# Masked layers of a cross-attention stack: a piece of work moves ahead of the scores in the pairs that follow a use of the scores' banks

## The chip, the cores and the metric

The kernel runs on one core of a Trainium2 chip. The metric is the device time of one execution in microseconds. Before the change the median of three runs is 4831.26 us (4831.16 to 4831.56). One more execution was profiled; its own time is 4829.9 us, and its span from the first to the last instruction is 4828.2 us. All work is in fp32, apart from a small bias term in bf16.

## The reference

The input is x with 2048 rows (queries) of 256 values, and a context of 1601 rows of 512 values. Four layers follow each other, and each adds to x what attention over the same context gives. Layers 0, 2 and 3 ("masked") have 16 heads of 64:

```
q = x @ Wq;  k = ctx @ Wk;  v = ctx @ Wv            # split into 16 heads of 64
logits = q k^T / 8 + col_bias                        # col_bias: up to -20 in four columns, by query
probs = softmax(logits)                              # over the 1601 keys
x = x + (probs v) @ Wo + bo
```

Layer 1 ("grouped") normalises x first and has 16 query heads of 16 values that share 4 key and value heads. The change does not touch its arithmetic.

## The kernel before

**Tiling.** A masked layer is cut into 8 blocks of two heads. In a block the 2048 queries are cut into 4 units of 512. So a masked layer has 32 units, and the three of them have 96. A unit works through the 1601 keys in 13 chunks (12 of 128 keys and one of 65). One chunk of one unit is a step. The scores of a step are keys by queries, for two heads: a tile of 128 x 1024 that fills two PSUM banks. The pool of these tiles (`psum.pair`, called `s` in the profile) has two of them.

**Three stages at once.** The main loop (line 1155) takes two steps at a time, which the text calls a pair. In a pair, three units are at work in different stages. For the newest one, `masked_scores` (line 681) computes scores on TensorE (L687, and L694 for the bias of the last chunk), ScalarE copies them to SBUF (L699), and VectorE keeps a running maximum over the chunks (L702 and L704, called `top`). Both read the tile of the scores, and the tile is free when both have done so. When a unit's 13 chunks are through, `maxima` (line 740) transposes the running maximum on TensorE into another tile of the scores' pool (L747), VectorE reduces it (L748), and two transfers spread the result over all partitions. For the unit before, 18 steps behind its scores, VectorE subtracts the maxima (L778), ScalarE takes exps (L783), and GpSimd adds them up (L786, L788). Its maxima are loaded into a PSUM tile by `maxima_spread` (L773) when it starts. Two steps behind the exps, `values` (line 808) multiplies by v on TensorE (L823).

**Pieces.** Everything else is cut into pieces that are put between the pairs (class `Pieces`, line 966). Each has a cost, and says whether it uses the PSUM bank that pieces share (`pm`). The fill pieces compute keys (L440) and values (L394) of the next block, 14 for a block of 26 pairs; each is followed by ScalarE's copy out of `pm`. Due pieces have a step at which they must run. A unit's queries (L464) are due at step 11 of the unit before. When a unit's values are complete, at step 6 of the second unit after it, `finish` (line 886) makes three more due: the denominators (L844 transposes the sums, L848 reduces them) two steps later, the division on GpSimd (L864) five steps later, and the project (L872, added to x by L884) ten steps later. Denominators and project use no `pm`, but a tile of the scores' pool; they are the ones that are marked `shared=False`.

`pair` (line 990) chooses for a pair of steps: it runs what is due (`own`, line 980), and if that cost nothing it takes one fill piece. The order of a pair in the program before is: the subtractions, the scores with copies and maxima, the exps, the values, then the pieces, and `maxima` where a unit's scores end. In the pair where a unit's values end on the first step, half of the values stands behind the piece.

**What sets the order.** The last lines of the function (1208 to 1214) chain the instructions of TensorE, ScalarE and VectorE in the order in which the program writes them. GpSimd and the queue of SyncE, which issues nearly all transfers, are not in that chain.

Two units take 26 steps, 13 pairs. In them two maxima, two denominators and two projects take a tile of the scores' pool.

Of the kernel before, what the change touches and what calls it, by code (L numbers as in the profile page):

```python
# [32 lines left out]

@with_exitstack
def tile_cross_attention_stack(ctx: ExitStack, tc: tile.TileContext, t: dict, out: bass.AP):

# [29 lines left out]
    x, cond = t["x"], t["ctx_2048"]  # L68
# [8 lines left out]
    NT = len(TCH)  # L77
# [22 lines left out]
    class Scores:  # L100
# [16 lines left out]
        def pair(self, shape=(2, QB)):  # L117
            return self.pairs.tile([P, *shape], FP, name="s")
# [40 lines left out]
    def key_order(tok):  # L159
# [27 lines left out]
        first = const.tile([P, NTOK], FP, name="first")  # L187
        keep = small.tile([P, NTOK], FP, name="keep", bufs=1)
        nc.vector.tensor_tensor(pair, across(tok), along(tok), ALU.is_equal)
        nc.vector.tensor_tensor(pair, pair, before, ALU.mult)  # L190
        nc.vector.tensor_reduce(first, pair, AX.X, ALU.max)
        nc.vector.tensor_scalar(first, first, 0.0, None, ALU.is_equal)
        nc.vector.scalar_tensor_tensor(first, tok, 0.0, first, ALU.is_ge, ALU.mult)
# [18 lines left out]
        def sources(a, b):  # L212
            n = b - a
            wide = [P, n, NTOK]

            def tokens_of(v):
                return v.rearrange("p (o j) -> p o j", o=1).to_broadcast(wide)

            def at_positions(v):
                return v.rearrange("p (n o) -> p n o", o=1).to_broadcast(wide)  # L220

            test = probs.tile(wide, FP, name="p")
            spec = probs.tile([P, n], FP, name="p")
            place = probs.tile([P, n], FP, name="p")
            to, at = src[:, a:b], pos[:, a:b]
            nc.vector.tensor_tensor(test, at_positions(at), tokens_of(where), ALU.is_ge)
            nc.vector.tensor_reduce(to, test, AX.X, ALU.add)
            nc.vector.tensor_tensor(to, to, at, ALU.add)

            nc.vector.tensor_scalar(place, at, count, float(T), ALU.add, ALU.subtract)  # L230
            nc.vector.scalar_tensor_tensor(to, place, 0.0, to, ALU.is_lt, ALU.mult)
            nc.vector.tensor_tensor(test, at_positions(place), tokens_of(rank), ALU.is_equal)
            nc.vector.tensor_tensor(test, test, tokens_of(mine), ALU.mult)
            nc.vector.tensor_reduce(spec, test, AX.X, ALU.add)
            nc.vector.tensor_tensor(to, to, spec, ALU.add)
# [713 lines left out]
    def first_unit(i):  # L949

        if i < NT / 2:
            first_block(i)
        if i == 1:
            layers[0].load_wo(made[0, 0])
            for b in range(NB):
                keep(0, b)
                pieces.at(2 * i + 2 + 2 * b, [(0, biases[b])])
        if i == 3:
            token_marks(0)
        if i == 7:  # L960
            small_constants()
            for l in range(1, NL):
                token_marks(l)
            start_block(0)

    class Pieces:
# [4 lines left out]
        def __init__(self):  # L971
            self.fill, self.later = deque(), deque()
            self.due = {}
            self.credit = 0.0

        def at(self, step, found):
            for steps, piece in found:
                self.due.setdefault(step + steps, []).append(piece)

        def own(self, steps):  # L980

            cost, taken = 0.0, False
            for step in steps:
                for piece in self.due.pop(step, ()):
                    piece.run()
                    cost += piece.cost
                    taken |= piece.shared and piece.cost > 0
            return cost, taken

        def pair(self, steps, pairs):  # L990

            cost, taken = self.own(steps)
            many = len(self.fill) + len(self.later) > pairs
            while self.fill and not taken and (many or not cost):
                piece = self.fill.popleft()
                piece.run()
                cost += piece.cost
                taken = piece.shared and piece.cost > 0

        def steps(self, steps, share):  # L1000


            self.credit = max(min(self.credit + share, 2.5), -2.5)
            cost, taken = self.own(steps)
            self.credit -= cost
            while self.fill and not taken and self.credit >= self.fill[0].cost / 2:
                piece = self.fill.popleft()
                piece.run()
                self.credit -= piece.cost
                taken = piece.shared and piece.cost > 0  # L1010
# [13 lines left out]
    pieces = Pieces()  # L1024
# [127 lines left out]
    def masked(unit):  # L1152
        return unit and unit.masked

    for first in range(0, N + NT + DELAY + LAG + 16, 2):
        pair = [Step(first), Step(first + 1)]

        if any(masked(x.scoring) for x in pair):
            if psum.banks:
                psum.by_pairs()  # L1160
        elif pair[0].exping and not pair[0].exping.masked and not psum.banks:
            psum.singly()

        kn, cn = divmod(first + 2 - NT - DELAY, NT)
        ahead = of[kn] if cn == 0 and 0 <= kn < len(units) and of[kn].masked else None
        three = not ahead and not any(masked(x.exping) for x in pair)
        for x in pair:
            x.begin()
        for x in pair:
            if masked(x.exping):  # L1170
                if x.cb == 0 and x is pair[1]:
                    x.exping.maxima_spread()
                x.exping.subtract(x.cb)
        for x in pair:
            if masked(x.scoring):
                x.scoring.masked_scores(x.ca)

        ends = all(masked(x.valuing) for x in pair) and pair[0].cv == NT - 1
        if ends:
            pair[0].valuing.values(NT - 1)  # L1180
        for x in pair:
            if masked(x.exping):
                x.exping.masked_exp(x.cb)
        if ahead:
            ahead.maxima_spread()
        if not ends:
            for x in pair:
                if masked(x.valuing):
                    x.valuing.values(x.cv)
        first_unit(first // 2)  # L1190
        together = masked(pair[0].scoring) and (masked(pair[1].exping) or not pair[1].exping)
        for x in pair:
            x.grouped(three)
            x.end()
            if not together:
                pieces.steps([x.step], x.share())
        if together:
            pieces.pair([first, first + 1], round(pair[0].units_left() * NT / 2))
        if ends:
            pair[1].valuing.values(0)  # L1200
        for x in pair:
            if x.scoring and x.ca == NT - 1:
                x.scoring.maxima()
                if not x.scoring.masked:
                    pieces.at(first + 2, [(0, Piece(x.scoring.maxima_rows, 0.3))])

# [41 lines left out]
```

## Time and profile before

| what | value |
|---|---|
| median of three runs | 4831.26 us |
| profiled execution: own time, span | 4829.9 us, 4828.2 us |
| TensorE matmul busy | 4667.0 us, 97% of the span |
| VectorE, ScalarE, GpSimd busy | 3746.8, 3225.1, 2991.6 us |
| idle TensorE ahead of scores L687 | 82.9 us |
| mean granted TensorE clock | 0.981 of full speed |

The masked layers take the profile from the start to about 1260 us and from about 2290 us to the end; between them lies the grouped layer. In the profile `s` is a tile of the scores' pool, `p` a tile of scores or probabilities in SBUF, `b` the maxima as `maxima_spread` puts them into PSUM, `pm` the bank of the pieces, `po` the values' output. A line of the timeline gives the start, the duration, the engine, the line of the kernel, the operation and its tiles, how many instructions are merged (x), and in brackets how long the engine was idle before and who released it. PEld is TensorE's weight load. A line of waits gives the total in us, how often, and the longest.

### The profile page before, as it was taken

Reading aid. Unit: us, or ns where it says so; the run is one execution under the profiler, and the core shown is the slowest. Engines: PE = TensorE matmul, PEld = TensorE weight load, DVE = VectorE, ACT = ScalarE, POOL = GpSimd, SP = SyncE. Lnnn points to the kernel's source line nnn. Section 1 sums busy time; section 2 is a strip of 40 time slices with the busy share of each in tenths; the row PEclk is TensorE's granted clock in tenths of the full one; section 3 lists DMA queues with packets and bytes.
Section 4 is the critical chain, followed back from the end, with each engine's and each line's share of the span. In section 5 each row is a group of like instructions: output and inputs, shape, how many; then the busy total and the mean of one; then the engine's idle time right before and its main releaser. Section 6 shows DMA issues by size and latency. Waiting matters only on the chain.

```text
span 4828.2 us, 64072 instructions
## 1 busy us (share of the span) xinstructions
PE 4667.0 (97%) x24020; PEld 1949.9 (40%) x24020; DVE 3746.8 (78%) x3766; ACT 3225.1 (67%) x4010; POOL 2991.6 (62%) x1440
## 2 busy tenths in 40 slices
PE   8999999999999999999999999999999999999996
PEld 5444444443433333343444444444444444444432
DVE  5888888888766666652678888888888888888886
ACT  5777777777545555544677777777777777777774
POOL 3777777778620000000577777777777777777787
PEclk9999999999889999998999999999999999999998
DMA  5322322222210000021232322322232222223201
GB/s 156 85 80 79 88 74 85 83 81 78 66 33 22 26 21 21 23 56 29 67 97 74 85 83 83 84 80 84 75 92 74 85 79 85 81 79 89 72 29 35
DMA packets 345990, 337.75 MB, mean 70 GB/s; under 512 B 112425, under 2 KB 301353, under 8 KB 345680
## 3 DMA queue, kind: packets, MB, share of 16 engines
q1 hardware_dynamic: 341984, 328.28, 23.8%
q8 instruction: 189, 3.10, 0.3%
q0 software_dynamic: 1152, 3.28, 0.2%
q10 hardware_dynamic: 2544, 2.10, 0.1%
q14 instruction: 121, 0.99, 0.1%
HBM read 318.76 MB, written 14.69 MB: 69 GB/s over the span
## 4 chain that ended last, share of the span: by engine, by line
PE 87%; DVE 10%; issue 1%; POOL 1%; ACT 1%; DMA 0%; POOLq 0%; ACTq 0%; DVEq 0%; SPq 0%
PE po L823 28%; PE s L687 20%; PE t L718 9%; PE pm L394 7%; PE pm L440 6%; PE s L872 4%; PE pm L464 4%; DVE ntop L748 2%; DVE rden L848 2%; PE s L844 2%; DVE xs L884 2%; PE s L747 2%; DVE top L704 1%; POOL sums L788 1%; PE t L793 1%
## 5 line engine op out<-in xcount | busy, mean ns | idle before, releaser
L788 POOL TENSOR_TENSOR sums<-sums,p 128x1024 f32<-128x1024 f32 (+1 forms) x1152 | 2726.4, 2367 | 741.0 <-ACT p L783 569.9
L699 ACT COPY p<-s 128x1024 f32<-128x1024 f32 (+1 forms) x1248 | 1234.7, 1014 | 665.7 <-PE s L687 573.5
L823 PE MATMUL po<-p,v 128*64 128x512 f32 (+3 forms) x8320 | 1506.7, 528 | 8.8 <-ACT p L783 5.8
L778 DVE TENSOR_TENSOR p<-p,b 128x1024 f32<-128x1024 f32 (+1 forms) x1248 | 1461.3, 1209 | 55.2 <-ACT b L773 52.9
L704 DVE TENSOR_TENSOR top<-s,top 128x1024 f32<-128x1024 f32 (+1 forms) x1056 | 1291.1, 1223 | 239.7 <-ACT p L699 176.7
L687 PE MATMUL s<-q,kT 64*128 64x512 f32 (+1 forms) x4992 | 1342.9, 632 | 82.9 <-DVE ntop L748 23.8
L783 ACT ACTIVATE p<-p 128x1024 f32<-128x1024 f32 (+1 forms) x1248 | 1254.8, 1057 | 49.1 <-DVE p L778 47.7
L823 PEld LDWEIGHTS po<-p,v 128*64 128x64 f32 (+3 forms) x8320 | 366.9, 126 | 1138.9 <-issue 905.4
L687 PEld LDWEIGHTS s<-q,kT 64*128 64x128 f32 (+1 forms) x4992 | 390.2, 182 | 721.1 <-issue 217.1
L805 ACT ACTIVATE p<-t 128x512 f32<-128x512 f32 (+1 forms) x760 | 413.7, 594 | 337.3 <-PE t L793 300.5
L731 DVE TENSOR_REDUCE row_top<-t 128x1 f32<-128x512 f32 x700 | 451.2, 686 | 215.7 <-PE t L793 186.6
L864 POOL TENSOR_TENSOR oT<-oT,by 128x512 f32<-128x512 f32 x112 | 142.9, 1276 | 719.4 <-DMA by<-cols 427.0
L793 PE MATMUL t<-q,kT 32*128 32x512 f32 (+1 forms) x1520 | 496.6, 656 | 0.0
L718 PE MATMUL t<-kT,q 32*128 32x512 f32 (+1 forms) x1880 | 490.1, 563 | 0.0
L394 PEld LDWEIGHTS pm<-wv,ct 128*128 128x128 f32 (+1 forms) x2600 | 300.4, 187 | 131.0 <-issue 68.4
L394 PE MATMUL pm<-wv,ct 128*128 128x128 f32 (+2 forms) x2600 | 333.3, 281 | 2.2 <-ACT v L398 0.9
L440 PE MATMUL pm<-ct,wk 128*128 128x256 f32 (+1 forms) x1344 | 314.5, 377 | 1.1 <-ACT ct L273 1.1
L748 DVE TENSOR_REDUCE ntop<-s 128x8 f32<-128x1024 f32 x96 | 117.6, 1225 | 232.8 <-PE s L747 232.8
L440 PEld LDWEIGHTS pm<-ct,wk 128*128 128x128 f32 x1344 | 230.8, 190 | 156.5 <-issue 101.0
L718 PEld LDWEIGHTS t<-kT,q 32*128 32x128 f32 x1880 | 183.7, 187 | 161.0 <-issue 94.1
L872 PE MATMUL s<-oT,wo 128*128 128x512 f32 x392 | 199.1, 631 | 15.1 <-POOL oT L864 11.1
L786 POOL COPY sums<-p 128x1024 f32<-128x1024 f32 x96 | 99.7, 1038 | 176.0 <-ACT p L783 176.0
(152 smaller groups left out, 2310.3 us busy)
## 6 DMA issues: line engine op xcount, KB each, us to landing
ct<-ctxT SPq DMA_DIRECT2D x288, 512.0 KB
xT<-xT SPq DMA_DIRECT2D x100, 512.0 KB
spread<-cols SPq DMA_DIRECT2D x96, 512.0 KB
by<-cols SPq DMA_DIRECT2D x192, 128.0 KB
xT<-xs SPq DMA_DIRECT2D x16, 512.0 KB
ct<-ctxT SPq DMA_DIRECT2D x48, 130.0 KB
wk<-in_L_xattn_Wk_dram SPq DMA_DIRECT2D x24, 256.0 KB
wv<-in_L_xattn_Wv_dram SPq DMA_DIRECT2D x24, 256.0 KB
```

What stands on the lines that cost most here:

```text
L394: nc.tensor.matmul(pv[:md, d, :f], ct(k)[:, d * P : d * P + md], wv[:, k, :], start=(k == 0), stop=(k == NCT - 1),)
L440: nc.tensor.matmul(pk, u.wk[:, k, :], ct(k), start=(k == 0), stop=(k == NCT - 1))
L687: nc.tensor.matmul(s[:m, h, :], self.u.kT[r, a : a + m], self.q[r, :], start=True, stop=(a != TAIL),)
L699: nc.scalar.copy(p[:m], s[:m])
L704: nc.vector.tensor_tensor(self.top[:m], s[:m], self.top[:m], ALU.max)
L718: nc.tensor.matmul(s[:, at : at + n], self.q[r, ts(q, P)], self.u.kT[r, a : a + n], start=True, stop=True,)
L731: nc.vector.tensor_reduce(self.top[:, of, q, k : k + 1], s, AX.X, ALU.max)
L778: nc.vector.tensor_tensor(self.p[c][:m], self.p[c][:m], self.less[:m], ALU.add)
L783: nc.scalar.activation(p[:m], p[:m], AF.Exp)
L788: nc.gpsimd.tensor_tensor(self.sums[:m], self.sums[:m], p[:m], ALU.add)
L793: nc.tensor.matmul(s[:m], self.u.kT[r, a : a + m], self.q[r, :], start=True, stop=True)
L823: nc.tensor.matmul(to, v, p, start=(c == 0 and not part), stop=(c == NT - 1 and part != 0))
```

## The change

The object `pieces` gets a flag, `scored`. It is set when a due piece runs that costs something and is not `shared` (denominators or project), and when `maxima` of a masked unit runs. At the start of the next pair, behind `begin`, the flag is read and cleared. If it was set and the pair is one of masked layers (`together`), the choice and the pieces that used to come at the pair's end run there, ahead of its subtractions and scores. If that cost something, nothing runs at the pair's end; else the choice is made at the end, as before. `own` now also takes what fell due at earlier steps, since a choice in front misses what becomes due later in its pair, and `pair` returns its cost.

```diff
@@ class Pieces
             self.due = {}
             self.credit = 0.0
+            self.scored = False
...
         def own(self, steps):
             cost, taken = 0.0, False
-            for step in steps:
-                for piece in self.due.pop(step, ()):
+            for step in sorted(step for step in self.due if step <= max(steps)):
+                for piece in self.due.pop(step):
                     piece.run()
                     cost += piece.cost
+                    self.scored |= piece.cost > 0 and not piece.shared
                     taken |= piece.shared and piece.cost > 0
             return cost, taken
...
                 taken = piece.shared and piece.cost > 0
+            return cost
@@ main loop
         for x in pair:
             x.begin()
+        together = masked(pair[0].scoring) and (masked(pair[1].exping) or not pair[1].exping)
+        steps, left = [first, first + 1], 0
+        if together:
+            left = round(pair[0].units_left() * NT / 2)
+        front = pieces.scored
+        pieces.scored = False
+        taken = pieces.pair(steps, left) if together and front else 0.0
...
         first_unit(first // 2)
-        together = masked(pair[0].scoring) and (masked(pair[1].exping) or not pair[1].exping)
         for x in pair:
             x.grouped(three)
             x.end()
             if not together:
                 pieces.steps([x.step], x.share())
-        if together:
-            pieces.pair([first, first + 1], round(pair[0].units_left() * NT / 2))
+        if together and not taken:
+            pieces.pair(steps, left)
...
                 x.scoring.maxima()
+                pieces.scored |= x.scoring.masked
```

## The prediction

> **What bounds the kernel now.** I read the page first: TensorE is busy nearly all the time, and the largest idle time in front of any of its groups stands before the scores of the masked layers (L687).
>
> ```profile
> PE 4667.0 (97%) x24020; PEld 1949.9 (40%) x24020; DVE 3746.8 (78%) x3766; ACT 3225.1 (67%) x4010; POOL 2991.6 (62%) x1440
> L687 PE MATMUL s<-q,kT 64*128 64x512 f32 (+1 forms) x4992 | 1342.9, 632 | 82.9 <-DVE ntop L748 23.8
> ```
>
> The waits of TensorE name three VectorE operations, each some 90 times, 0.26 us a time: maxima, denominators, projections.
>
> ```profile
> PE s L687 <- DVE ntop L748: 23.8, 92, 0.3
> PE s L687 <- DVE rden L848: 22.2, 87, 0.3
> PE s L687 <- DVE xs L884: 22.0, 85, 0.3
> ```
>
> The chain that ended last shows the same thing as a detour through VectorE, between two scores of one pair.
>
> ```profile
> 3064.68 0.02 issue
> 3064.70 1.24 DVE xs L884
> 3065.94 0.04 issue
> 3065.98 1.13 PE s L687 x4
> ```
>
> The timeline of two neighbouring pairs has what I need for prices; the second begins at 3040.39.
>
> ```profile
> 3035.11 2.34 DVE L778 TENSOR_TENSOR p<-p,b 128x1024 f32<-128x1024 f32 x2
> 3035.43 1.99 PE L687 MATMUL s<-q,kT 64*128 64x512 f32 x8
> 3036.66 1.93 ACT L699 COPY p<-s 128x1024 f32<-128x1024 f32 x2 [0.75 <-PE s L687]
> 3037.35 1.94 PE L823 MATMUL po<-p,v 128*64 128x512 f32 x8
> 3037.71 2.55 DVE L704 TENSOR_TENSOR top<-s,top 128x1024 f32<-128x1024 f32 x2 [0.26 <-ACT p L699]
> 3039.22 1.24 PE L844 MATMUL s<-ident,sums 128*128 128x128 f32 x8
> 3040.39 1.13 PE L687 MATMUL s<-q,kT 64*128 64x512 f32 x4
> 3040.49 1.23 DVE L848 TENSOR_REDUCE rden<-s 128x8 f32<-128x1024 f32 x1 [0.23 <-PE s L844]
> 3041.77 1.13 PE L687 MATMUL s<-q,kT 64*128 64x512 f32 x4 [0.26 <-DVE rden L848]
> 3041.87 2.30 DVE L778 TENSOR_TENSOR p<-p,b 128x1024 f32<-128x1024 f32 x2
> ```
>
> By starts (ends of matmuls are modelled), a pair is scores 1.92, values 1.87, and one piece: keys 1.93, values' projection 1.98, queries 1.92, project 1.91, denominators 1.17, maxima about 1.0. Behind denominators, project or maxima the second scores wait: 6.24 between pair starts (3052.66 to 3058.90) instead of 1.93 + 1.92 + 1.87 = 5.72. So a stall costs **0.52**: 0.26 shown idle, the rest drain and refill.
>
> The same lines show what limits the banks. A copy L699 starts 1.23 after its scores and takes 1.01; L704 starts 0.04 after that copy; then a bank is free. In the last block, where nothing is left to fill with, values are followed directly by denominators, and these wait for it:
>
> ```profile
> 4667.51 1.94 PE L823 MATMUL po<-p,v 128*64 128x512 f32 x8
> 4669.94 1.21 PE L844 MATMUL s<-ident,sums 128*128 128x128 f32 x8 [0.49 <-DVE top L704]
> 4671.17 1.13 PE L687 MATMUL s<-q,kT 64*128 64x512 f32 x4
> ```
>
> They start 2.43 after the values instead of 1.87. This is the picture that the change will make common.
>
> **What the skill says.** The Trainium skill, "PSUM — Partial Sum Buffer", section Terms: ScalarE and VectorE must not use one bank at once, reads against reads included. The trace agrees: no L704 starts before its copy has ended, even where VectorE is idle. "Perfetto Trace Analysis", section "Tensor Engine Instruction (MATMUL, LD_WEIGHTS)": matmul ends are estimates; hence starts here (x8 scores read 1.99, the next group starts after 1.92). "PSUM", section "Engine vs sequencer instructions": ScalarE's and VectorE's queues are strict first in, first out; so in their written order a late operation delays all behind it.
>
> **The change, part by part.** No instruction is added or removed. After a pair that took the scores' banks at its end, the next pair's piece (TensorE matmuls, ScalarE's evacuation of 0.37 or 0.60) runs ahead of that pair's scores, and nothing runs at its end. Two units are 13 pairs (77.88 from 3004.01 to 3081.89). By steps within a unit: project is due at 3, denominators at 8, queries at 11, maxima at 12. I number the pairs P0 to P12, P0 holding steps 0 and 1 of a unit that starts on an even step. In front come the pieces of P0, P2, P5 (queries), P7, P9, P11. Seven fill pieces meet seven places, as before; only the place within the pair moves. The evacuation ends 2.40 (queries 2.62) after the pair's start, before the first score copy at 3.16: hidden. If that cover failed, each 0.1 would delay both copies by 0.1.
>
> *Gain:* six stalls of 0.52, 3.1 a cycle. *Where it goes:* a front pair makes its scores 1.93 later, so copies and tops come later, while the pair itself has become shorter and the next pair's scores follow its values with no piece between. I follow this from the front pair's start.
>
> P7 and P8 (values' projection in front, project behind). VectorE: reduction 0.10 to 1.33, subtractions ready at 3.59. TensorE: piece to 1.98, scores to 3.90, values to 5.77. First copy 3.21 to 4.22; tops 4.26 to 6.81. P8's first scores start at 5.77, its second would at 6.73, but the second bank is free at 6.81: start 6.86 and a refill of 0.10 (after such waits values follow 1.06 behind, not 0.96): 0.23 late. VectorE then subtracts (from 6.71, first top 2.26 later since the operations overlap by 0.1) and ends P8's first top at 10.19. Project would start at 5.77 + 0.23 + 3.79 = 9.79; its bank allows 10.34 (in the last block such starts are 0.15 behind the top). Queued behind it on TensorE are P9's front piece and scores; all shift with it, and nothing else is late. It ends at 10.34 + 1.89 = 12.23. Before: 6.29 + 5.70 = 11.99. **+0.24**.
>
> P9 and P10: the same with denominators, 1.24 to the next start: 11.58 against 6.30 + 4.96 = 11.26. **+0.32**.
>
> P0 and P1: chunk 0 has no top, so P0's only top ends at 6.39, P1's first at 9.77, project starts at 9.92, ends 11.81. Before: 6.24 + 5.69 = 11.93. **-0.12**.
>
> P2 and P3: P2 loads the maxima (L773) between its two subtractions. VectorE's chain (reduction, subtraction, L773, subtraction, tops) ends at 7.30 after P2's start now, and it is just as long afterwards. P3's values start at 7.35 + 1.06 = 8.41; now 3073.00 - 3064.59 = 8.41. **0**.
>
> P11 and P12: the piece is the short last one (1.02). Tops end at 6.30, second scores start at 6.35; now 6.30. **0** within 0.05.
>
> P4 to P6: P5 becomes 5.70 from 6.23; P6 pays 0.12, for its second scores would start at 6.78 and the bank is ready at 6.80. **-0.41**, the one place where the stall goes, because P6 has a fill piece ahead of its maxima.
>
> Sum: +0.24 + 0.32 - 0.12 + 0 + 0 - 0.41 = **+0.03 a cycle**. The masked layers have 96 units, 48 cycles; the last block has no fill pieces, the first block fewer: 45 count, +1.4 us. On the profiled execution (4828.2 span, 4829.9) that is 4831.3; the median lies 1.4 higher: 4832.7, say **4832**.
>
> The rest costs nothing. GpSimd needs 4.8 of 5.7 us a pair for the sums; the division (1.28) may stand ahead of P5's sums, but they are needed two pairs later. If it did hold them that long, score copies would wait for their p buffers, as the 44.7 us in all do now. SyncE issues the context slices when a slot comes free, three pieces ahead; a piece that comes 3.8 us earlier still finds its slice. The orders of SyncE and GpSimd are not fixed by the written order (a division at 3049.89 ran ahead of sums written before it), so they may shift: bounded by 0 and by some ten waits of 1 us each.
>
> What is unknown is the balance. Each 0.05 in the copy's 1.23, which enters three doubles and P6, is 0.2 a cycle: 9 us either way.
>
> **Rivals.**
> - *Full gain:* banks come free in time and the stalls go: 45 x 3.1 = 140 us, 4691. For it: the stall is real, and pieces do cover it. Against: tops would have to end 0.15 sooner in front pairs, and first tops behind them 0.7 sooner. 0.05.
> - *Part of it:* waits of 0.23 and 0.55 come out shorter by 0.1 to 0.2 each (a top overlapping more with what is ahead of it): 0.3 to 1.0 a cycle, 4787 to 4821. 0.23.
> - *Slower:* ScalarE hands its copies over late. In the pair behind a front pair the first copy is due at 7.00, and the exps of the front pair end only at about 7.1. If in front pairs the first copy starts later than 3.2 by d, both waits grow by d; it decides from d = 0.06 (0.06 x 4 x 45 = 10 us), and d = 0.2 gives +36, 4868. 0.24.
> - *It does nothing:* with the fill queue empty nothing comes in front, as in the last block; this falls under no change.
>
> **How the numbers follow.** The stalls moving to the next bank, with the sum as worked out: 0.48, 4822 to 4841. 0.2% is 9.7 us, about what a measurement of this kernel can tell from no change. Faster: 0.05 + 0.23 = 0.28; same 0.48; slower 0.24. Leaving out the full gain and half of each tail: 4802 to 4862.
>
> **What would show it.** Waits of scores for ntop, rden and xs should fall from some 264 to those of the last block and the few pairs without fill; in their place waits of L872 and L844 for the tops of about 0.5 us appear some 130 times, and scores wait for tops by 0.1 to 0.4. Front pairs last 5.7, pairs behind them that end in project 6.1 to 6.5. Wrong if L872 and L844 start right behind the values (full gain), or if copies in front pairs start over 1.3 after their scores (slower).

## The result, and the profile after

The changed kernel takes 4808.34 us (4806.61 to 4813.06, five runs), against 4831.26 us before (4829.69 to 4831.56, five runs). The ratio is 0.9955, with a 95% interval of 0.9941 to 0.9970: 0.45% or 23 us faster. The forecast was 4832 us, its range 4802 to 4862, and its likeliest case a change too small to measure. The time lies in the range, but that case did not come true. The profiled execution spans 4805.6 us, 22.6 us less than the one of before (4828.2).

The page of the changed kernel, its busy times and its group of scores (all lines of the masked layers' code stand one line further down than before: L688 is the old L687):

```profile
PE 4593.8 (96%) x24020; PEld 1956.3 (41%) x24020; DVE 3742.6 (78%) x3766; ACT 3214.2 (67%) x4010; POOL 2996.8 (62%) x1440
L688 PE MATMUL s<-q,kT 64*128 64x512 f32 (+1 forms) x4992 | 1310.3, 627 | 66.6 <-DVE top L705 57.2
```

TensorE executes the same 24020 matmuls in 73.2 us less busy time (4667.0 before), at the same mean clock of 0.981. The idle time ahead of the scores fell only from 82.9 to 66.6 us. Not all of the 73.2 us is shorter work: of a stall of 0.52 us the profile showed only 0.26 as idle, and the rest counted as busy. The starts below sort this out, and they too say that most of the gain is work that became shorter. The forecast had no term for that.

The waits of TensorE in the changed kernel (total in us, times, longest):

```profile
PE s L688 <- DVE top L705: 57.2, 188, 1.6
PE s L873 <- DVE top L705: 35.2, 88, 0.5
PE s L845 <- DVE top L705: 22.7, 47, 0.5
```

Before, scores waited 264 times for `ntop`, `rden` and `xs`, 0.26 us each, 68.0 us together. Here are the waits that the forecast put in their place: project (L873) and denominators (L845) wait 88 + 47 = 135 times for a top (some 130 were forecast), 0.40 and 0.48 us in the mean.

The chain that ended last, between the scores of a front pair and the project of the next:

```profile
3015.87 1.23 DVE top L705
3017.09 0.06 DVE p L779
3017.16 0.98 issue
3018.14 1.21 DVE p L779
3019.35 1.15 DVE top L705
3020.49 0.14 issue
3020.63 1.95 PE s L873 x4
```

Where it went before from TensorE to one VectorE operation and back, it now follows ScalarE and VectorE for some seven microseconds (3013.41 to 3020.63) and returns to TensorE when a top has freed project's bank.

The timeline of TensorE in one stretch, P7 to the front of P9 and, below it, the end of P10 and the front of P11 (the numbering of pairs is that of the prediction):

```profile
3009.41 1.13 PE L748 MATMUL s<-ident,top 128*128 128x128 f32 x8
3010.38 1.95 PE L395 MATMUL pm<-wv,ct 128*128 128x128 f32 x16
3012.26 1.99 PE L688 MATMUL s<-q,kT 64*128 64x512 f32 x8
3014.18 1.94 PE L824 MATMUL po<-p,v 128*64 128x512 f32 x8
3016.05 2.23 PE L688 MATMUL s<-q,kT 64*128 64x512 f32 x8
3018.21 1.94 PE L824 MATMUL po<-p,v 128*64 128x512 f32 x8
3020.63 1.95 PE L873 MATMUL s<-oT,wo 128*128 128x512 f32 x4 [0.48 <-DVE top L705]
3022.42 1.95 PE L395 MATMUL pm<-wv,ct 128*128 128x128 f32 x16
3024.30 1.99 PE L688 MATMUL s<-q,kT 64*128 64x512 f32 x8
...
3032.67 1.21 PE L845 MATMUL s<-ident,sums 128*128 128x128 f32 x8 [0.49 <-DVE top L705]
3033.72 1.04 PE L395 MATMUL pm<-wv,ct 128*65 128x128 f32 x8
3034.68 1.99 PE L688 MATMUL s<-q,kT 64*128 64x512 f32 x8
```

The waits are those of the forecast to a hundredth or two. P8's scores take 2.16 from start to start (3016.05 to 3018.21) instead of 1.92: 0.24 late, where 0.23 was forecast. Project would follow the values by 1.87, at 3020.08, and starts at 3020.63: 0.55 late, as forecast. But every matmul group that touches the new place is shorter than the price that the forecast had for it. Project to the piece behind it takes 1.79 (the sum had 1.89), the values' projection to the scores 1.88 (1.98), denominators to the piece 1.05 (1.24).

Over two units of 13 pairs, from the start of one P5 to the start of the next, the windows add up so (the first of these lines is the kernel before, the second the changed one; `sum` is the stretch, then the busy time of each engine in it):

```profile
sum 77.88, PE 76.33 PEld 32.13 DVE 65.89 ACT 56.61 POOL 61.22; mean PE 10.90 PEld 4.59 DVE 9.41 ACT 8.09 POOL 8.75
```

```profile
sum 76.96, PE 74.59 PEld 32.32 DVE 65.78 ACT 56.37 POOL 61.34; mean PE 10.66 PEld 4.62 DVE 9.40 ACT 8.05 POOL 8.76
```

TensorE idles more now (76.96 - 74.59 = 2.37 us against 1.55), and still the cycle is 0.92 shorter, because the busy time fell by 1.74. (Ends of matmuls are modelled, so only the sign of this split is to be trusted; the 0.92 comes from starts.)

### The profile page after: what moved, and what is told of

Read it like the earlier page. It is cut to its first block, busy times and chain, and to the rows that moved or that the text cites. A ratio compares the mean times of both kernels' runs of the same rounds, so it can differ in the third digit from the quotient of the medians.

```text
span 4805.6 us, 64046 instructions
## 1 busy us (share of the span) xinstructions
PE 4593.8 (96%) x24020; PEld 1956.3 (41%) x24020; DVE 3742.6 (78%) x3766; ACT 3214.2 (67%) x4010; POOL 2996.8 (62%) x1440
## 4 chain that ended last, share of the span: by engine, by line
PE 62%; DVE 22%; ACT 6%; issue 6%; POOL 2%; DMA 1%; DVEq 0%; SPq 0%; ACTq 0%; POOLq 0%
PE po L824 15%; PE s L688 12%; DVE top L705 11%; PE t L719 9%; DVE p L779 6%; PE pm L395 5%; ACT p L700 5%; PE pm L441 4%; PE s L873 4%; PE pm L465 3%; PE s L845 2%; DVE top L703 2%; PE s L748 2%; POOL sums L789 2%; DVE xs L885 1%
## 5 line engine op out<-in xcount | busy, mean ns | idle before, releaser
L700 ACT COPY p<-s 128x1024 f32<-128x1024 f32 (+1 forms) x1248 | 1222.1, 1018 | 349.5 <-PE s L688 271.6
L688 PE MATMUL s<-q,kT 64*128 64x512 f32 (+1 forms) x4992 | 1310.3, 627 | 66.6 <-DVE top L705 57.2
L688 PEld LDWEIGHTS s<-q,kT 64*128 64x128 f32 (+1 forms) x4992 | 401.8, 182 | 795.8 <-DVE top L705 429.2
L395 PE MATMUL pm<-wv,ct 128*128 128x128 f32 (+2 forms) x2600 | 323.6, 277 | 3.1 <-ACT v L399 1.8
L873 PE MATMUL s<-oT,wo 128*128 128x512 f32 x392 | 200.0, 634 | 54.7 <-DVE top L705 35.2
L399 ACT COPY v<-pm 128x256 f32<-128x256 f32 (+1 forms) x168 | 59.8, 356 | 274.7 <-PE pm L395 274.7
```

Source lines behind the costliest of these rows:

```text
L395: nc.tensor.matmul(pv[:md, d, :f], ct(k)[:, d * P : d * P + md], wv[:, k, :], start=(k == 0), stop=(k == NCT - 1),)
L688: nc.tensor.matmul(s[:m, h, :], self.u.kT[r, a : a + m], self.q[r, :], start=True, stop=(a != TAIL),)
L700: nc.scalar.copy(p[:m], s[:m])
```

## What the experiments had to tell apart

*Theory A, tile shapes.* The scores' matmuls have 64 rows (64*128 in the profile), the values' matmuls 128*64, and the pieces 128*128 (128*65 in the last chunk). TensorE loses time when the shape changes from one group to the next. A piece put directly behind another piece saves one change there and back. The Trainium skill, "TensorEngine Tiling (Array Packing)", section Tiling Modes, under Key Properties, says that a change of tiling mode, in contrast to a change of the tile alone, drains TensorE. The runs below show a loss of time at such a change; that it is a drain, none of them shows. I had not drawn on the page for the forecast. The trace of before already had its size, in rows that I passed over: the same queries, once with scores behind them and once with the maxima.

```profile
3008.32 1.98 PE L464 MATMUL pm<-xT,wq 128*128 128x512 f32 x4
3010.24 1.08 PE L687 MATMUL s<-q,kT 64*65 64x512 f32 x4
...
3049.78 1.98 PE L464 MATMUL pm<-xT,wq 128*128 128x512 f32 x4
3051.61 1.12 PE L747 MATMUL s<-ident,top 128*128 128x128 f32 x8
```

Queries to scores takes 1.92, queries to maxima 1.83. In the changed kernel the group in front of the queries is a 128*128 one and the scores follow: 1.81 (2997.90 to 2999.71). So a change of shape costs some 0.1 us on the group before it and up to 0.1 on the group after it.

*Theory B, waits alone.* A piece costs what it cost before, whatever stands beside it, and what was gained was gained where waits for the scores' banks became shorter.

The expectations give numbers for both. "Cycle" below is the time of 13 pairs, taken from the starts of scores two units apart in the steady part of the trace; cycles with values' pieces and with keys' pieces alternate. They are 77.70 and 78.00 us before and 76.84 and 77.02 after; apart from those where a layer begins or ends, most cycles of a kind agree within 0.03 us. How much falls to each of two neighbouring cycles depends, by 0.1 us or so, on where in the unit the starts are taken, so their mean is the better measure: 77.85 before, 76.93 after.

## The three places one by one

Each of these kernels is the changed one with the flag set behind one kind of bank-taking piece only.

```diff
 # maxima alone: in own
-                    self.scored |= piece.cost > 0 and not piece.shared
 # denominators alone: in own, and at the end of the main loop
-                    self.scored |= piece.cost > 0 and not piece.shared
+                    self.scored |= piece.cost == 1.0 and not piece.shared
-                pieces.scored |= x.scoring.masked
 # projects alone
-                    self.scored |= piece.cost > 0 and not piece.shared
+                    self.scored |= piece.cost == 2.0 and not piece.shared
-                pieces.scored |= x.scoring.masked
```

> The flag is set behind maxima alone; pieces behind denominators and projects stay at the end of their pair. Theory A (the waits as the prediction summed them, and besides some 0.1 us saved wherever two groups of 128 rows stand side by side on TensorE, because the step from 128 rows to the 64-row scores is then paid once instead of twice): 4 to 5 us faster than before, 4826. Theory B (no such saving, waits alone): 6 us slower, 4837. Waits of scores for ntop gone, those for rden and xs left as before.

> The flag is set behind denominators alone. In one of two places no bank is taken in the next pair but one, in the other a short piece leads to VectorE's chain. Theory A: 24 us faster than before, 4807, as much as the whole change. Theory B: 18 us faster, 4813.

> The flag is set behind projects alone. One of its two front pairs runs into the denominators' wait for a top, the other into VectorE's chain with the loading of the maxima. Theory A: 7 us slower than before, 4838. Theory B: 12 us slower, 4843. If the change gains because every covered stall is a gain, it would be about 8 us faster.

| front piece behind | ratio (95%) | cycles, us | against before |
|---|---|---|---|
| maxima | 0.9984 (0.9976 to 0.9993) | 77.44, 77.61 | -0.26, -0.39 |
| denominators | 0.9933 (0.9920 to 0.9946) | 77.07, 77.36 | -0.63, -0.64 |
| projects | 1.0001 (0.9993 to 1.0010) | 77.75, 78.04 | +0.05, +0.04 |
| all three (the change) | 0.9955 (0.9941 to 0.9970) | 76.84, 77.02 | -0.86, -0.98 |

In the cycles the three parts add up: -0.84 and -0.99 against -0.86 and -0.98, in the mean -0.92 against -0.92. Two of the expectations of A came close in the whole time (4.5 us faster for maxima, measured by the ratio 0.16% or 8 us; 24 us faster for denominators, measured 0.67% or 32 us), but projects, which A had 7 us slower and B 12, make no difference. The expectations of B put maxima on the slower side, which the interval excludes. The expectation of B for denominators, 18 us faster, lies outside its interval as well. This is evidence for A, not proof: the three differ in the waits too. With maxima alone project waits 88 times for a top, 0.40 us in the mean, with projects alone the denominators wait 48 times, 0.48 us, and with denominators alone hardly anything waits in this way, 9 times in all. In the whole time denominators alone do as well as all three, though their cycle gains less; the time outside the cycles is taken up below.

## A shape in between: four kernels with one small matmul more

To measure the change of shape by itself, a dummy matmul is put between the bank-taking piece and the front piece, once with 64 rows and once with 128. Its result is read by nobody, and all of the computation remains. The kernel with 64 rows does half the multiplications; by A it is the dearer one, since it brings a change of shape on either side of it, and the other brings none.

In the first pair of kernels the dummy had a `pm` tile of its own (here with 64 rows; in the other `ident[:128, :]` and `ident[:128, :64]`):

```diff
+        if together and front:
+            pd = ps_m.tile([P, QB], FP, name="pm")[:, :64]
+            nc.tensor.matmul(pd, ident[:64, :], ident[:64, :64], start=True, stop=True)
         taken = pieces.pair(steps, left) if together and front else 0.0
```

> The change, with one more matmul of 64 rows and 64 columns (a part of the identity by a part of the identity, result unused) between the piece that took the banks and the piece in front: the shape of the scores put between two groups of 128 rows. Theory A, now sharper: each switch of TensorE between shapes costs about 0.1 at the last matmul before it and 0.05 to 0.1 at the first one after it, and the change's gain is that it leaves out one switch in each of six places of two units. Then this matmul adds two switches in each place, 0.3 to 0.4 us: with its own 0.06 some 1.8 us per two units, about 80 us slower than the change, 50 to 60 slower than before. Theory B, the 0.1 belongs to the wait on the scores' banks or to something else that scores alone do: 6 to 12 us slower than the change, like the one with 128 rows.

> The same with 128 rows and 64 columns: no switch is added, the matmul takes 0.1 or so, some 0.5 us per two units. Both theories: 10 to 25 us slower than the change. Against the one with 64 rows, theory A: 60 to 70 us faster, though it does more; theory B: no difference, or a few us slower.

Measured: 64 rows 4946.07 us, ratio 1.0217 (1.0202 to 1.0233); 128 rows 4897.37 us, 1.0119 (1.0103 to 1.0134). The difference, 49 us or 1.1 us a cycle, has the sign of A but is smaller than expected, and both kernels are slower than expected. The traces show why: the front piece had to wait until the dummy's tile was free (it starts 0.49 behind the start of the 64-row dummy and 0.40 behind the 128-row one), and this wait covers a part of the change of shape. The pair was therefore made anew, with the dummy written into the tile that the front piece then overwrites, so that no wait comes with it. `between` is called first thing in the pieces of values, keys and queries:

```diff
+        between(pv[:, 3, :64])
...
+    def between(to):
+        while extra:
+            extra.pop()
+            nc.tensor.matmul(to, ident[:64, :], ident[:64, :64], start=True, stop=True)
@@ main loop
+        extra[:] = [1] if together and front else []
         taken = pieces.pair(steps, left) if together and front else 0.0
+        extra[:] = []
```

> As the matmul of 64 rows and 64 columns before, but it writes into the tile of the piece in front, so that the piece does not wait for it (in the runs before that wait took 0.33 us and hid a part of the switch). Theory A (switches between shapes): the last matmul of the group before grows by 0.1, the first of the piece by 0.05 to 0.1, and the small one itself lasts some 0.2: 0.3 to 0.4 us in each of six places of two units, 1.2 to 1.8 us per two units slower than the change. Theory B (the 0.1 belongs to the scores' waits): 0.1 us a place, 0.6 per two units.

> The same with 128 rows and 64 columns. Both theories: about 0.1 us a place, 0.3 to 0.6 us per two units slower than the change, with neighbours as long as in the change (project's last matmul 0.43, the first of a values' projection 0.11). Theory A: 0.8 to 1.2 us per two units faster than with 64 rows, theory B: no faster.

The 64-row kernel takes 4911.95 us, ratio 1.0158 (1.0140 to 1.0177), with cycles of 79.24 and 79.46. The 128-row kernel takes 4846.96 us, ratio 1.0020 (1.0011 to 1.0028), with cycles of 77.72 and 77.90. The timelines, first with 64 rows (project is L882 in these two kernels, the dummy L410, scores L697):

```profile
3030.60 1.96 PE L882 MATMUL s<-oT,wo 128*128 128x512 f32 x4 [0.31 <-DVE top L714]
3032.48 0.43 PE L410 MATMUL pm<-ident 64*128 64x64 f32 x2
3032.84 2.05 PE L397 MATMUL pm<-wv,ct 128*128 128x128 f32 x16
3034.83 1.99 PE L697 MATMUL s<-q,kT 64*128 64x512 f32 x8
```

And with 128 rows:

```profile
3044.59 1.95 PE L882 MATMUL s<-oT,wo 128*128 128x512 f32 x4 [0.48 <-DVE top L714]
3046.38 0.33 PE L410 MATMUL pm<-ident 128*128 128x64 f32 x2
3046.55 2.00 PE L397 MATMUL pm<-wv,ct 128*128 128x128 f32 x16
3048.48 1.99 PE L697 MATMUL s<-q,kT 64*128 64x512 f32 x8
```

From start to start, project, dummy and piece take 1.88, 0.36 and 1.99 with the 64-row dummy, and 1.79, 0.17 and 1.93 with the 128-row one. Together 4.23 against 3.89: the smaller matmul costs 0.34 us more. All three groups are longer, the one ahead of the dummy as well as the one behind it. Matmul by matmul, the last one of project takes 0.52 instead of 0.43 from start to start, and the first one of the piece 0.21 instead of 0.17. The matmuls, their order and the tiles are otherwise the same in both kernels, no wait stands between them, and the wait of project comes before these starts. It is no single place: behind maxima and denominators and with each kind of piece the medians differ by 0.32 to 0.34 us, at some 245 of the 256 dummies.

In whole cycles the two kernels differ by 1.54 us, in the whole time by 65 us. The sum of the 256 places would be some 84 us; a part of the rest shows in the scores' waits for tops, which are 16 us shorter in all with the 64-row dummy (21.0 against 36.9). Both kernels are dearer than expected, 2.42 and 0.88 us a cycle above the change where 1.2 to 1.8 and 0.3 to 0.6 were expected, and their difference of 1.54 is above A's 0.8 to 1.2. Theory B, which had 64 rows no dearer than 128, has no place for it; it falls, and the cost of a change of shape is measured by itself.

The loads of the weights (PEld) show one thing that goes with it. First with 64 rows, then with 128:

```profile
3032.48 0.29 PEld L410 LDWEIGHTS pm<-ident 64*128 64x128 f32 x2 [0.76 <-issue]
3032.84 1.86 PEld L397 LDWEIGHTS pm<-wv,ct 128*128 128x128 f32 x16
```

```profile
3045.95 0.19 PEld L410 LDWEIGHTS pm<-ident 128*128 128x128 f32 x1 [0.24 <-issue]
3046.38 0.19 PEld L410 LDWEIGHTS pm<-ident 128*128 128x128 f32 x1 [0.24 <-issue]
3046.49 1.87 PEld L397 LDWEIGHTS pm<-wv,ct 128*128 128x128 f32 x16
```

The weights of the 128-row dummy are loaded at 3045.95, with the start of project's last matmul and 0.43 us ahead of the dummy (3046.38). Those of the 64-row dummy are loaded at 3032.48, together with the dummy itself. The traces of before and after say the same of the groups that follow each other without a wait in the second and third masked layer: at a change of shape the load starts with its own matmul (2 or 3 ns ahead of it in the median; scores of 65 and of 128 columns count as one shape), from one 128*128 group to another it starts 0.11 to 0.43 us ahead. So at a change of shape the next weights are not loaded while the matmul before is still at work. Whether this is the whole of the loss, no run separates.

## The piece between the two scores

If the front piece stood between the first and the second scores, the bank would be ready for the second scores, and the tops of the first would not come later. The choice was the change's, but the piece was put behind the first scores of its pair, unless one that takes the scores' banks was due.

```diff
-        taken = pieces.pair(steps, left) if together and front else 0.0
+        front = front and together
+        banks = any(p.cost > 0 and not p.shared for s in pieces.due if s <= steps[1] for p in pieces.due[s])
+        taken = pieces.pair(steps, left) if front and banks else 0.0
...
                 x.scoring.masked_scores(x.ca)
+            if x is pair[0] and front and not banks:
+                taken = pieces.pair(steps, left)
```

> As the change, but the piece that comes in front stands between the pair's first and second scores, unless it takes a bank itself. The first copy and top are then not late, the second scores still find their bank emptied, but the step from 128 rows to the scores is paid twice. Theory A: 41 us faster than before, 4790: waits of project and denominators for tops shrink from 0.5 to some 0.2 to 0.4. If late copies were not what makes the tops late, it would be no better than the change, and slower by 0.1 for each step from 128 rows to scores, 270 of them, 27 us.

Measured: 4824.99 us, ratio 0.9973 (0.9962 to 0.9983), 13 us faster by the ratio where some 41 were expected; cycles 77.29 and 77.57. The waits did what was wanted. Project and denominators:

```profile
PE s L873 <- DVE top L705: 23.7, 89, 0.5
PE s L845 <- DVE top L705: 12.5, 46, 0.5
```

They are as many as in the changed kernel, but 0.27 us each. What the expectation had counted too low is in the timeline; it had one more change of shape for each such place:

```profile
3016.22 1.12 PE L748 MATMUL s<-ident,top 128*128 128x128 f32 x8
3017.27 1.13 PE L688 MATMUL s<-q,kT 64*128 64x512 f32 x4
3018.33 2.05 PE L395 MATMUL pm<-wv,ct 128*128 128x128 f32 x16
3020.31 1.13 PE L688 MATMUL s<-q,kT 64*128 64x512 f32 x4
3021.37 1.94 PE L824 MATMUL po<-p,v 128*64 128x512 f32 x8
```

Half of the scores, alone between groups of another shape, takes 1.06 where two halves together take 1.92, and the piece takes 1.98 again, its full price. Here the shape changes at each of the four boundaries from maxima to values, in the changed kernel at two (maxima to piece does not count, piece to scores and scores to values do). So there are two more changes of shape for each such place, not one. This kernel has the shorter waits and the longer cycle.

## Taking away the waits that came instead

The 0.55 ahead of project and denominators has a removable cause: VectorE makes both subtractions of a pair before the first top, and the bank that project needs is freed by that top. In the pair behind a front pair, the second subtraction now comes after the first scores' top.

```diff
+        between = behind and not taken and together and pair[1].cb != 0 and masked(pair[0].exping)
+        behind = taken > 0
         for x in pair:
-            if masked(x.exping):
+            if masked(x.exping) and not (between and x is pair[1]):
...
                 x.scoring.masked_scores(x.ca)
+            if between and x is pair[0]:
+                pair[1].exping.subtract(pair[1].cb)
```

> The change, and in the pair behind a front pair VectorE takes the first top ahead of its second subtraction. If project and denominators wait because VectorE reaches their top late (two subtractions stand ahead of it), their waits of 0.5 shrink to 0.1 or go: 0.4 to 0.6 us per two units, 20 to 28 us faster than the change, 4785. If the copies were late instead, no difference.

Measured: 4784.89 us, ratio 0.9882 (0.9867 to 0.9897). The time is the expected one, but the kernel before took 4838.95 us in this comparison, so it is the ratios that count: they put this kernel 26 to 35 us ahead of the change (0.9936 in its second comparison, given below, and 0.9955). Cycles are 76.20 and 76.38, 0.64 us shorter than with the change, where 0.4 to 0.6 were expected. Of the 135 waits for tops ahead of project and denominators six are left. The scores still wait for tops, 189 times and 70.3 us in all, 13 us more than with the change.

The last kernel adds what the three single places had shown, that a front piece behind a project gains nothing by itself: the flag is set behind maxima and denominators only.

```diff
-                    self.scored |= piece.cost > 0 and not piece.shared
+                    self.scored |= piece.cost == 1.0 and not piece.shared
```

> The same, with the flag set behind maxima and denominators alone, since the project's front pairs gained nothing by themselves. Per two units 0.3 us less than with the flag behind all three: 32 us faster than the change, 4776. If the gains are additive only without the new order of VectorE, it is equal to the one with all three.

Measured: 4758.17 us, ratio 0.9836 (0.9822 to 0.9849): 1.6% faster than the kernel before, faster than the changed one too. Cycles are 75.90 and 76.08. The timeline around one project in this kernel, of VectorE and TensorE:

```profile
2991.10 1.21 DVE L779 TENSOR_TENSOR p<-p,b 128x1024 f32<-128x1024 f32 x1
...
2992.30 1.94 PE L824 MATMUL po<-p,v 128*64 128x512 f32 x8
2992.41 1.23 DVE L705 TENSOR_TENSOR top<-s,top 128x1024 f32<-128x1024 f32 x1
...
2993.55 1.21 DVE L779 TENSOR_TENSOR p<-p,b 65x1024 f32<-65x1024 f32 x1
...
2994.16 1.98 PE L873 MATMUL s<-oT,wo 128*128 128x512 f32 x4
```

The top that frees project's bank ends at 2993.64, before the values have done, and project follows them by 1.86 without a wait. Leaving projects out brought 0.30 us a cycle, as expected. In the whole time the medians of the two kernels are 27 us apart, where 9 were expected and 45 such cycles make 14; the four runs of the kernel with projects lie up to 16 us apart, so the rest may be spread. The stretch from the scores of P8 to those of P12 carries the 0.30 (22.46 us in the kernel with projects, 22.16 in this one); with projects in front, the scores of P12 come 0.61 later behind those of P11 (4.71 against 4.10), and wait longer for a top. Why the third place costs more in this company than alone (0.05 a cycle) was not followed further.

## The change a second time

The cycles alone would make 45 x 0.92 = 41 us, and the comparison gave 23. So the change was timed again.

> The change as it is, to compare its whole time with its cycles. The steady cycles of its trace are 0.92 us shorter than those of the kernel before, and 45 of them count: 41 us, against 23 us in the comparison on record. If the difference of 18 us belongs to the change (pairs outside the steady cycles that became longer), this run shows 0.9953 again, about -23 us; if it is the spread from run to run outside the steady cycles (begin of the first masked layer, grouped layer, begin of the second), this run shows between -30 and -41 us, 0.9915 to 0.9938. Each cycle itself is to be 76.84 and 77.02 us again, within 0.03.

Measured: 4801.9 us against 4831.03, ratio 0.9936 (0.9922 to 0.9949), 29 us or 31 by the ratio; its cycles are 76.83 and 77.01. So 6 to 8 us of the 18 missing are spread from run to run, and 10 to 12 remain. The steady cycles cannot hold them. The traces put most of them at the very start, ahead of the first piece that moved. The first 460 matmuls stand in the same order in both kernels; the last of them starts at 109.5 us before, and at 117.8 and 118.3 in the two profiles of the changed kernel. The 8 to 9 us are lost between 23 and 42 us: TensorE is busy for all 19 us there in the trace of before, at full clock, and for 14.5 and 13.8 us, at a mean granted clock of 0.73, in the other two, where it stands still once for 4.3 and 5.0 us. All kernels made from the changed one have such a stop (3.6 to 6.5 us), and there is one trace of the kernel before, so whether the changed program or that one execution is the exception stays open; the pieces that moved are not the cause, since none has moved yet. A smaller part may sit where the second masked layer begins: its first four units take 148.3 us before, 152.0 and 150.9 in the two profiles of the changed kernel, and anything from 150 to 159 in the others.

## Why the prediction was wrong, and where it was right

*The waits: right.* That the stalls would not vanish but move to the next user of a bank; where (second scores of the pair behind, project, denominators); how long (0.23 and 0.55 forecast, 0.24 and 0.55 measured); and how many (130 against 135): all this the profile shows as worked out (project behind P1 is the exception that the working had too, 0.38 late for 0.41). Of what was costed at nothing, nothing else became visible in the cycles: copies of front pairs start 1.23 after their scores (3012.26 to 3013.49), so the slower rival did not come.

*The prices of TensorE's pieces: wrong.* The step that failed is the working of the pairs in the part on the change. It took each piece's duration from a row in which the next group is scores (keys 1.93, values' projection 1.98, queries 1.92, project 1.89, denominators 1.16 and, from the last block, 1.24) and carried it to a place where another 128*128 group stands before or behind it. By steps, with starts from the timelines of both kernels:

| pairs | before | forecast | measured | what was mis-sized |
|---|---|---|---|---|
| P7, P8 | 11.99 | +0.24 | 12.04, +0.05 | piece 1.88 for 1.98, project 1.79 for 1.89 |
| P9, P10 | 11.26 | +0.32 | 11.30, +0.04 | piece 1.88 for 1.98, denominators 1.05 for 1.24 |
| P11, P12 | 12.27 | 0 | 12.27, 0 | right; shorter pieces (0.96, 0.97) disappear in the waits for tops |
| P0, P1 | 11.93 | -0.12 | 11.57, -0.36 | keys 1.82 for 1.93, project 1.80 for 1.89 |
| P2, P3 | 12.36 | 0 | 12.44, +0.08 | right within 0.08: VectorE's chain sets it |
| P4 to P6 | 18.07 | -0.41 | 17.34, -0.73 | denominators 1.08 for 1.16, queries 1.81 for 1.92, maxima 0.97 for 1.07 |
| sum | 77.88 | +0.03 | 76.96, -0.92 | |

Six places with two boundaries of 0.1 each would be 1.2 us; the two pairs of pairs where VectorE's chain is the longer one keep their length, and 0.95 against the forecast is what remains. With 0.1 taken off at each boundary but there, the same sum would have given about -0.9 a cycle, 41 us and 4790, too low in the whole time by 12 to 18 us, of which most lies at the start of the program and in the spread from run to run, as told above.

*The rivals.* "Part of it" named 4787 to 4821 (its 0.3 to 1.0 a cycle make 4787 to 4819), and 4808 lies in it. That is luck, for its mechanism is not what happened: it had the waits shorter by 0.1 to 0.2, and they are not. What it called a gain of 0.3 to 1.0 a cycle came from the work around the waits. "Full gain" and "it does nothing" are excluded by the waits of L873 and L845.

*The chances.* The prediction named as unknown only the delay of the copy. That a price itself could depend on the neighbour was in the trace of before (1.83 against 1.92) and had no case of its own: 0.1 at each boundary would have made "faster" the likeliest.

## What to carry to other kernels

When work is moved, take its price from a row with the same neighbours, not only with the same instructions: on TensorE a group that gets a neighbour of its own tile shape is about 0.1 us shorter at that side. Put groups of one shape together where the order is free, and when a wait moves to the next user of a bank, look at the order of the operations on the engine that frees it: moving one VectorE operation behind another was worth 0.64 us a cycle here, against the 0.92 of the change itself.

## What the runs showed of the hardware

One 64-row matmul between two 128-row groups costs 0.34 us more than one of 128 rows in the same place, though it does half the work, and a group of four scores alone between other shapes takes 1.06 us where eight take 1.92. The loss falls on the last matmul before the change (project's 0.52 for 0.43) and on the first after it (the dummy's 0.16 for 0.06), about 0.1 us each, and the load of the next weights does not start ahead there, as it does between groups of one shape. The profile does not show the loss as idle time: TensorE counts as busy in it. The page's share of busy TensorE (97% before) therefore contained time that an order of the work could free.
